# Deformable sampling in a four-layer network: gathered rows as the stationary operand, corner weights as the moving one

## The chip, the cores and the metric

The kernel runs on one core of a Trainium2 chip. A core has engines that run side by side, each through its own list of instructions in order: TensorE for matrix products (PE in the profile; PEld is its loading of the stationary operand), VectorE (DVE), ScalarE (ACT), GpSimd (POOL) and SyncE (SP), which here only starts DMAs. They wait for each other through semaphores. A matrix product takes a stationary operand, which is loaded into the array first, and a moving operand, which is streamed through it column by column; the sum over partitions lands in PSUM[...]. The result's partitions are the columns of the stationary operand, and its columns are those of the moving one.

The metric is the device time of one execution in microseconds (us). Lower is better.

## The reference

Four images of 256 channels and 64x64 pixels go through four layers, each added to its input. Layer 0 holds the part that changes: a deformable convolution. For every pixel, each of four groups of 64 channels has nine points with offsets computed from the data; the image is read at each point by bilinear interpolation (four corners), and the nine values are summed with a softmax mask.

```python
inp = y.transpose(0, 2, 3, 1)
xp = jnp.einsum('nhwc,oc->nhwo', inp, inproj_w) + inproj_b
offset = jnp.einsum('nhwc,oc->nhwo', t, off_w) + off_b
mask = jax.nn.softmax(mlog.reshape(n, H, W, G, P), -1).reshape(n, H, W, G * P)
...
samp = _grid_sample(img, sg)
mr = mask.reshape(n, H * W, G, P).transpose(0, 2, 1, 3).reshape(n * G, 1, H * W, P)
dout = (samp * mr).sum(-1).reshape(n, G * GC, H * W).transpose(0, 2, 1).reshape(n, H, W, C)
dout = jnp.einsum('nhwc,oc->nhwo', dout, outproj_w) + outproj_b
x2 = _bn(inp + dout, bn2_g, bn2_b, bn2_m, bn2_v, 3)
```

So for one pixel and one group the sampling is a sum of 9 points x 4 corners = 36 rows of 64 channels, each times one number (mask times bilinear weight). The rest is dense: 1x1 convolutions and a feed-forward block in layer 0, linear attention with a 5x5 depthwise convolution in layer 1, a binary 3x3 convolution in layer 2, and attention against a pooled image in layer 3.

## The kernel before

`run` lays the four images out as a pipeline. `sample(n)` is the sampling of image n, and is the backbone of four stages: sampling 0 beside the convolutions and offsets of images 1 to 3; sampling 1 beside the feed-forward (`feed`) and layer 1 (`linear`) of image 0; sampling n (2 and 3) beside `feed` and `linear` of image n-1 and layers 2 and 3 (`second`) of image n-2. What is left of images 2 and 3 comes after as a tail without sampling. All these are Python generators, and `beside` interleaves them by hand: after each step of the sampling it advances the others by their share of estimated cost. Within the stages, `ordered()` makes the order of the program the order on TensorE, VectorE, ScalarE and GpSimd. Nothing is rearranged at run time: an instruction that waits holds back all that stand behind it on its engine.

The sampling goes by *rounds* of 14 pixels (`RP`), each with nine points, so 126 of 128 partitions hold one (pixel, point) pair. 293 rounds make an image. Two rounds make a *unit* (`UR`), four share one tile of weights (`WR`), and sixteen are a *block* (`BR`) of 224 pixels, after which the output projection runs.

- `load` (L572) brings a block's table indices and corner weights into `sl` by two DMAs of SP.
- `weigh` (L583) spreads the weights on VectorE into `wm`: for each (pixel, point) row and each group and corner, 16 columns (`OB`) that are zero but for the row's own pixel. So a product of `wm` with gathered rows sums the nine points of every pixel.
- `gathered` (L596) starts four indirect DMAs on GpSimd (L600), one for each group. Each brings to every partition one row of 256 numbers: four corners of 64 channels. The tile `g` has seven buffers. Then eight matmuls follow (L607), for two pairs of corners `x` and four groups `i`, with two corners and 16 columns of `wm` as the stationary operand (128 rows x 32 columns) and two corners' channels of `g` as the moving one (128 columns). Group i's sum goes to partitions 32i to 32i+31 of the accumulator `acc`: pixels (for two corners) in partitions, channels in columns. Of the 32x128 results of a group, those where the stationary's corner is the moving's corner are of use. Each fp32 matmul shows as two passes in the profile, so sixteen records a round.
- `moved` (L610) copies a unit's accumulator from PSUM to SBUF (`at`, ScalarE, L612).
- `turned` (L614) transposes each round's 128x128 on TensorE into a second PSUM bank, `dp` (L617), which puts channels into partitions.
- `spread` (L619) copies the useful halves on ScalarE (L632) from `dp` to `dT`, where all of a block's pixels lie side by side.
- `project` (L636), `add` and `finish` (L642 to L649) are the output projection of the block from `dT`, the sum with the image, and the batch norm.

The main loop (L654 on) issues the matmuls of a round, and puts off what follows: `todo` gives each of `moved`, `turned` and `spread` a step at which it is issued. For a unit whose last round is step i these are i+1, i+2 and i+3 (i+4 in a block's first unit). PSUM is shared out by names: `acc` and `dp` are one bank each, of two halves used in turn by units:

```python
        def halves(name):

            t = self.ps1.tile([P, 2, 256], F32, name=name, tag=name)
            return cycle([t[:, 0], t[:, 1]])

        accs, dps = halves("acc"), halves("dp")
```

The framework derives the waits from tiles, and both halves of a bank are one tile. In the tail the two banks serve other work.

Of the kernel before, what the change touches and what calls it, by code (L numbers as in the profile page):

```python
# [9 lines left out]
F32 = mybir.dt.float32  # L10
# [7 lines left out]
P = 128  # L18
# [5 lines left out]
G, PT = 4, 9  # L24
# [5 lines left out]
RP, WR, UR, BR = 14, 4, 2, 16  # L30
RS, BP = RP * PT, RP * BR
BLOCKS = [(p0, min(BP, HW - p0)) for p0 in range(0, HW, BP)]
OB = 16
# [38 lines left out]
class Net:  # L72
# [483 lines left out]
    def sample(self, n, ssum):  # L556

        nc, sp = self.nc, self.sp
        table = self.tab[n].rearrange("g y x s c -> (g y x) (s c)")
        blocks, images, at, dp, dT, po, later = {}, {}, {}, {}, {}, {}, {}

        def halves(name):

            t = self.ps1.tile([P, 2, 256], F32, name=name, tag=name)
            return cycle([t[:, 0], t[:, 1]])

        accs, dps = halves("acc"), halves("dp")  # L570

        def load(b):  # L572
            p0, np_ = BLOCKS[b]
            whole, part = np_ // RP, np_ % RP

            nr = whole + (part > 0)
            sl = sp.tile([P, BR, G * 5], F32, name="sl")
            rows = self.s_d[n][p0 * PT:p0 * PT + nr * RS, :].rearrange("(r p) f -> p r f", p=RS)
            more = self.s_d[n][p0 * PT + RS:p0 * PT + (nr + 1) * RS, :].rearrange("(r p) f -> p r f", p=RS)
            nc.sync.dma_start(sl[0:RS, 0:nr], rows)  # L580
            nc.sync.dma_start(sl[RS:P, 0:nr], more[0:P - RS])
            rounds = [(r, RP) for r in range(whole)] + [(whole, part)] * (part > 0)
            blocks[b] = sl, rounds  # L583

        def weigh(b, r):

            sl, rounds = blocks[b]
            nu = min(WR, len(rounds) - r)
            wm = self.gp.tile([P, WR, 4 * G, OB], F32, name="wm")
            sh = [P, nu, 4 * G, OB]  # L590
            nc.vector.tensor_tensor(  # L591
                wm[:, 0:nu], self.con("own").unsqueeze(1).unsqueeze(1).to_broadcast(sh),
                sl[:, r:r + nu, G:].unsqueeze(3).to_broadcast(sh), ALU.mult)
            return wm

        def gathered(sl, wm, acc, r):  # L596
            r4, acc = r % WR, acc[:, r % UR * P:(r % UR + 1) * P]
            g = self.gp.tile([P, G, 256], F32, name="g", bufs=7)
            for i in range(G):
                nc.gpsimd.indirect_dma_start(  # L600
                    out=g[:, i, :], out_offset=None, in_=table,
                    in_offset=bass.IndirectOffsetOnAxis(ap=sl.bitcast(I32)[:, r, i:i + 1], axis=0))


            for x in range(2):
                for i in range(G):
                    nc.tensor.matmul(acc[32 * i:32 * i + 32, :], wm[:, r4, 4 * i + 2 * x:4 * i + 2 * x + 2, :],  # L607
                                     g[:, i, x * P:(x + 1) * P], start=x == 0, stop=x == 1)

        def moved(acc, nu, u):  # L610
            at[u] = sp.tile([P, UR, P], F32, name="at")
            nc.scalar.copy(at[u].rearrange("p v c -> p (v c)")[:, 0:nu * P], acc[:, 0:nu * P])  # L612

        def turned(nu, u):  # L614
            dp[u] = next(dps).rearrange("p (v g s o) -> p v g s o", v=UR, g=G, s=2)
            for v in range(nu):
                nc.tensor.transpose(dp[u][:, v].rearrange("p g s o -> p (g s o)"), at[u][:, v], self.ident)  # L617

        def spread(unit, b, u):  # L619

            if b not in dT:
                p0, np_ = BLOCKS[b]
                dT[b] = sp.tile([P, G, BP], F32, name="dT", bufs=1)
                images[b] = sp.tile([P, KT, BP], F32, name="yb")
                nc.sync.dma_start(images[b][:, :, 0:np_], self.y_d[n][:, :, p0:p0 + np_])
            full = sum(1 for _, m in unit if m == RP)
            for v0, v1, m in ((0, full, RP), (full, len(unit), unit[-1][1])):
                for s in range(2):
                    if v0 < v1:
                        hs = slice(64 * s, 64 * s + 64)  # L630
                        q0 = RP * (unit[0][0] + v0)
                        nc.scalar.copy(  # L632
                            dT[b][hs, :, q0:q0 + m * (v1 - v0)].rearrange("p g (v o) -> p g v o", o=m),
                            dp[u][hs, v0:v1, :, s, 0:m].rearrange("p v g o -> p g v o"))

        def project(b, m):  # L636
            np_ = BLOCKS[b][1]
            po[m] = self.ps("po")
            for k in range(G):
                nc.tensor.matmul(po[m][:, 0:np_], self.ow[:, k, m * P:(m + 1) * P], dT[b][:, k, 0:np_], start=k == 0, stop=k == G - 1)  # L640

        def add(b, m):  # L642
            ym = images[b][:, m, 0:BLOCKS[b][1]]
            nc.vector.tensor_tensor(ym, po[m][:, 0:BLOCKS[b][1]], ym, ALU.add)

        def finish(b, m):
            p0, np_ = BLOCKS[b]
            ym = images[b][:, m, 0:np_]
            nc.scalar.activation(ym, ym, AF.Identity, bias=self.sh[:, 4 + m:5 + m],  # L649
                                 scale=self.inv[:, 4 + m:5 + m], accum_out=ssum[:, m, b:b + 1])  # L650
            if m == KT - 1:
                nc.sync.dma_start(self.x2_d[n][:, :, p0:p0 + np_], images[b][:, :, 0:np_])

        load(0)  # L654
        order = [(b, r) for b, (_, np_) in enumerate(BLOCKS) for r in range(-(-np_ // RP))]
        wm = weigh(0, 0)
        for i, (b, r) in enumerate(order):
            for f in later.pop(i, ()):
                f()
            sl, rounds = blocks[b]  # L660
            if r % UR == 0:
                acc = next(accs)
            gathered(sl, wm, acc, r)
            if r == 0 and b + 1 < len(BLOCKS):
                load(b + 1)
            ends = r + 1 == len(rounds)
            if r % WR == 0:
                if r + WR < len(rounds):
                    nxt = weigh(b, r + WR)
                elif b + 1 < len(BLOCKS):  # L670
                    nxt = weigh(b + 1, 0)
            if r % UR == UR - 1 or ends:
                unit = rounds[r - r % UR:r + 1]
                todo = [partial(moved, acc, len(unit), i), partial(turned, len(unit), i), partial(spread, unit, b, i)]

                todo = [(i + 1 + j + (j == 2 and r < UR), f) for j, f in enumerate(todo)]
                if ends:
                    todo += [(i + 4 + m + j, partial(f, b, m)) for m in range(KT) for j, f in enumerate((project, add, finish))]
                for j, f in todo:
                    later.setdefault(j, []).append(f)  # L680
            if r % WR == WR - 1 or ends:
                wm = nxt
            yield 1
        for i in sorted(later):
            for f in later[i]:
                f()
# [656 lines left out]
```

## Time and profile before

| | before |
|---|---|
| median of 3 runs | 8817.04 us (8797.73 to 8818.68) |
| span of the profiled execution | 8805.8 us |
| mean granted TensorE clock | 0.809 of full |
| DMA | 1042.27 MB, mean 118 GB/s |
| first and last matmul of the sampling start at | 139.6 and 7330.2 us |
| first matmul of the sampling of images 0, 1, 2, 3 | 140, 1951, 3718, 5537 us |

Of the granted clock the records know two values, half and full, so a mean of 0.809 says for what share of the time it was full. A line of groups reads: source line, engine, operation, output<-inputs by the program's names, shape (stationary and moving operands for TensorE), count | busy us, mean ns of one | idle us of the engine just before them, and what ended most of it. In a line of the timeline, the brackets at the end hold the idle time before and what ended it; "remote" is a semaphore that was raised where no record of another engine ends, and "issue" is time in which the engine waited for nothing that the profile shows. A line of waits gives the us in total, the times and the longest.

### The profile page before, as it was taken

How to read it: one execution, taken by the hardware profiler on the slowest of the kernel's cores; microseconds unless marked ns; L12 is line 12 of the kernel's file. 1: busy time of each engine (PE TensorE's matmuls, PEld its weight loads, DVE VectorE, ACT ScalarE, POOL GpSimd, SP SyncE). 2: the span in 40 equal slices, each digit the busy share in tenths (PEclk: the TensorE clock that was granted, in tenths of full speed). 3: DMA queues.
4: the chain of work that ended last, by engine and by line, in shares of the span. 5: the costliest groups of instructions: out<-in, count | busy, mean ns of one | idle time of the engine just before them, and what ended most of it. 6: DMA issues, size and time to landing. Idle time of an engine off the chain costs nothing. (4 is left out here: it accounts for less than half of the span.)

```text
span 8805.8 us, 95736 instructions
## 1 busy us (share of the span) xinstructions
PE 5993.9 (68%) x36532; PEld 3575.6 (41%) x36532; DVE 5173.3 (59%) x6409; ACT 2183.8 (25%) x4899; POOL 5152.4 (59%) x4950
## 2 busy tenths in 40 slices
PE   4454554448744446688876677888766778986899
PEld 2222222224323322244544443345544433664477
DVE  5444443443466667424777776227777772599834
ACT  1111111112211112122223222222222222465524
POOL 2666666566666666666666656666666661376410
PEclk7676766669866667799988888898878888998999
DMA  6454454444433334444443344444434343220131
GB/s 172 127 155 124 141 154 118 125 145 145 153 105 105 110 105 129 127 130 138 134 135 110 112 121 136 142 134 132 136 115 117 114 118 99 69 74 29 48 98 53
DMA packets 759050, 1042.27 MB, mean 118 GB/s; under 512 B 362432, under 2 KB 472128, under 8 KB 757056
## 3 DMA queue, kind: packets, MB, share of 16 engines
q0 software_dynamic: 225024, 614.77, 24.3%
q1 hardware_dynamic: 533568, 421.39, 16.4%
q8 instruction: 289, 4.73, 0.2%
q14 instruction: 169, 1.38, 0.0%
HBM read 867.08 MB, written 168.69 MB: 118 GB/s over the span
## 5 line engine op out<-in xcount | busy, mean ns | idle before, releaser
L600 POOL DMA_INDIRECT g<-tab,sl x4688 | 4618.5, 985 | 2687.8 <-issue 1224.2
L178 DVE SCALAR_TENSOR_TENSOR agg<-pad,vec,agg 128x1024 f32<-128x1024 f32 x2280 | 2933.5, 1287 | 61.9
L607 PE MATMUL acc<-g,wm 128*32 128x128 f32 x18752 | 1034.8, 333 | 1907.8 <-ACT at L612 1273.7
L607 PEld LDWEIGHTS acc<-g,wm 128*32 128x32 f32 x18752 | 566.8, 128 | 2411.7 <-ACT at L612 1446.1
L1048 PE MATMUL ps<-xd,w 128*128 128x256 f32 x3072 | 752.7, 396 | 51.3 <-issue 37.8
L591 DVE TENSOR_TENSOR wm<-con,sl 128x1024 f32<-128x1024 f32 (+1 forms) x296 | 357.7, 1209 | 711.9 <-remote 533.5
L1048 PEld LDWEIGHTS ps<-xd,w 128*128 128x128 f32 x3072 | 595.1, 199 | 175.0 <-issue 86.0
L632 ACT COPY dT<-dp 64x112 f32<-64x112 f32 x1176 | 285.9, 243 | 1043.7 <-remote 544.3
L742 PE MATMUL ps<-x2f,f 128*128 128x512 f32 x1024 | 499.2, 636 | 19.1 <-issue 7.7
L817 PE MATMUL ps<-xr,qw 128*128 128x512 f32 x768 | 472.0, 746 | 22.1 <-issue 11.1
L727 DVE SCALAR_TENSOR_TENSOR hm<-ps,vec,lk 128x512 f32<-128x512 f32 x256 | 190.8, 750 | 492.9 <-ACT lk L744 405.5
L752 PE MATMUL ps<-hm,f 128*128 128x512 f32 x1024 | 467.1, 605 | 0.9 <-DVE hm L727 0.9
L612 ACT COPY at<-acc 128x256 f32<-128x256 f32 (+1 forms) x588 | 218.3, 371 | 986.3 <-remote 753.2
L999 POOL TENSOR_TENSOR xd<-xp 128x640 f32<-128x640 f32 x64 | 79.4, 1268 | 492.6 <-ACT xp L1011 298.3
L640 PE MATMUL po<-dT,ow 128*128 128x224 f32 (+1 forms) x1216 | 326.1, 419 | 45.4 <-issue 19.3
L617 PE MATMUL dp<-ident,at 128*128 128x128 f32 x1172 | 284.1, 330 | 106.6 <-ACT dT L632 61.0
L865 ACT COPY kt<-pt 128x512 f32<-128x512 f32 x256 | 149.4, 584 | 829.3 <-remote 403.8
L744 ACT ACTIVATE lk<-ps,low 128x512 f32<-128x512 f32 x256 | 174.0, 687 | 666.0 <-PE ps L742 512.1
L1147 PE MATMUL s<-ph,th 128*128 128x512 f32 x512 | 290.2, 672 | 62.5 <-ACT kt L865 15.9
L640 PEld LDWEIGHTS po<-dT,ow 128*128 128x128 f32 x1216 | 265.5, 233 | 113.8 <-issue 68.9
L1167 PEld LDWEIGHTS ps<-gt,pT 128*128 128x128 f32 x2048 | 276.0, 213 | 70.8 <-issue 46.1
L194 POOL TENSOR_TENSOR ak<-ak,m 128x1024 f32<-128x1024 f32 x96 | 228.1, 2376 | 130.6 <-ACT m L193 126.7
(243 smaller groups left out, 8022.0 us busy)
## 6 DMA issues: line engine op xcount, KB each, us to landing
g<-tab,sl POOLq DMA_INDIRECT x4688
x<-x SPq DMA_DIRECT2D x128, 512.0 KB
xr<-x SPq DMA_DIRECT2D x96, 512.0 KB
tab<-xo SPq DMA_DIRECT2D x192, 128.0 KB
x<-in_x SPq DMA_DIRECT2D x32, 512.0 KB
y<-yc SPq DMA_DIRECT2D x32, 512.0 KB
x2f<-x SPq DMA_DIRECT2D x32, 512.0 KB
xyf<-x SPq DMA_DIRECT2D x32, 512.0 KB
```

Source lines behind the costliest of these rows:

```text
L178: nc.vector.scalar_tensor_tensor(to, s, wt, acc, ALU.mult, ALU.add)
L591: nc.vector.tensor_tensor(wm[:, 0:nu], self.con("own").unsqueeze(1).unsqueeze(1).to_broadcast(sh), sl[:, r:r + nu, G:].unsqueeze(3).to_bro ...
L600: nc.gpsimd.indirect_dma_start(out=g[:, i, :], out_offset=None, in_=table, in_offset=bass.IndirectOffsetOnAxis(ap=sl.bitcast(I32)[:, r, i: ...
L607: nc.tensor.matmul(acc[32 * i:32 * i + 32, :], wm[:, r4, 4 * i + 2 * x:4 * i + 2 * x + 2, :], g[:, i, x * P:(x + 1) * P], start=x == 0, st ...
L617: nc.tensor.transpose(dp[u][:, v].rearrange("p g s o -> p (g s o)"), at[u][:, v], self.ident)
L632: nc.scalar.copy(dT[b][hs, :, q0:q0 + m * (v1 - v0)].rearrange("p g (v o) -> p g v o", o=m), dp[u][hs, v0:v1, :, s, 0:m].rearrange("p v g ...
L640: nc.tensor.matmul(po[m][:, 0:np_], self.ow[:, k, m * P:(m + 1) * P], dT[b][:, k, 0:np_], start=k == 0, stop=k == G - 1)
L742: nc.tensor.matmul(ps, f1[:, k, m * P:(m + 1) * P], x2[:, k], start=k == 0, stop=k == KT - 1)
L752: nc.tensor.matmul(ps, f2[:, k, m * P:(m + 1) * P], hm[:, k], start=k == 0, stop=k == 4 * KT - 1)
L817: nc.tensor.matmul(ps, qw[:, k, m * P:(m + 1) * P], x[:, k], start=k == 0, stop=k == KT - 1)
L1048: nc.tensor.matmul(ps[:, e], w[:, k, t, 2 * half + e, m * P:(m + 1) * P], v[:, 2 * half + e, k, t:t + 8], start=i % 6 == 0, stop=i % 6 == 5)
L1147: nc.tensor.matmul(s[i], tv[:, 4 * b + j], ph[:, i * 512:(i + 1) * 512], start=True, stop=True)
```

## The change

The two operands of the sampling's matmul change places. The gathered rows of one group and one pair of corners (128 rows x 128 columns) are loaded as the stationary operand, and the 32 columns of `wm` move. The sum then comes out with corners and channels in partitions and pixels in columns, which is the layout that `turned` made. So `moved` and `turned` go, and `spread` reads the accumulator itself. A round now fills 4 groups x 32 = 128 columns on all 128 partitions. The order of the loops turns from corner pairs outside to groups outside, so that the two matmuls that add up into one place follow each other. The two PSUM banks both serve as accumulators, each in two halves, and successive units take a half of `acc`, a half of `dp`, the other half of `acc`, the other half of `dp`. `spread` is issued at the same step as before. Gathers, weights, projection and everything beside the sampling are unchanged.

```diff
-        blocks, images, at, dp, dT, po, later = {}, {}, {}, {}, {}, {}, {}
-
-        def halves(name):
-
-            t = self.ps1.tile([P, 2, 256], F32, name=name, tag=name)
-            return cycle([t[:, 0], t[:, 1]])
-
-        accs, dps = halves("acc"), halves("dp")
+        blocks, images, dT, po, later = {}, {}, {}, {}, {}
+        banks = [self.ps1.tile([P, 2, UR, G, 2, OB], F32, name=tag, tag=tag) for tag in ("acc", "dp")]
+        accs = cycle([t[:, i] for i in range(2) for t in banks])
...
-            r4, acc = r % WR, acc[:, r % UR * P:(r % UR + 1) * P]
+            r4, acc = r % WR, acc[:, r % UR]
...
-            for x in range(2):
-                for i in range(G):
-                    nc.tensor.matmul(acc[32 * i:32 * i + 32, :], wm[:, r4, 4 * i + 2 * x:4 * i + 2 * x + 2, :],
-                                     g[:, i, x * P:(x + 1) * P], start=x == 0, stop=x == 1)
-
-        def moved(acc, nu, u):
-            at[u] = sp.tile([P, UR, P], F32, name="at")
-            nc.scalar.copy(at[u].rearrange("p v c -> p (v c)")[:, 0:nu * P], acc[:, 0:nu * P])
-
-        def turned(nu, u):
-            dp[u] = next(dps).rearrange("p (v g s o) -> p v g s o", v=UR, g=G, s=2)
-            for v in range(nu):
-                nc.tensor.transpose(dp[u][:, v].rearrange("p g s o -> p (g s o)"), at[u][:, v], self.ident)
-
-        def spread(unit, b, u):
+            for i in range(G):
+                for x in range(2):
+                    nc.tensor.matmul(acc[:, i], g[:, i, x * P:(x + 1) * P],
+                                     wm[:, r4, 4 * i + 2 * x:4 * i + 2 * x + 2, :], start=x == 0, stop=x == 1)
+
+        def spread(acc, unit, b):
...
-                            dp[u][hs, v0:v1, :, s, 0:m].rearrange("p v g o -> p g v o"))
+                            acc[hs, v0:v1, :, s, 0:m].rearrange("p v g o -> p g v o"))
...
-                todo = [partial(moved, acc, len(unit), i), partial(turned, len(unit), i), partial(spread, unit, b, i)]
-
-                todo = [(i + 1 + j + (j == 2 and r < UR), f) for j, f in enumerate(todo)]
+                todo = [(i + 3 + (r < UR), partial(spread, acc, unit, b))]
```

## The prediction

> **What bounds the kernel now.** I read the page first: the busy shares, then the slices, then the groups of the sampling lines.
>
> ```profile
> PE 5993.9 (68%) x36532; PEld 3575.6 (41%) x36532; DVE 5173.3 (59%) x6409; ACT 2183.8 (25%) x4899; POOL 5152.4 (59%) x4950
> ...
> POOL 2666666566666666666666656666666661376410
> PEclk7676766669866667799988888898878888998999
> ...
> L600 POOL DMA_INDIRECT g<-tab,sl x4688 | 4618.5, 985 | 2687.8 <-issue 1224.2
> ...
> L607 PE MATMUL acc<-g,wm 128*32 128x128 f32 x18752 | 1034.8, 333 | 1907.8 <-ACT at L612 1273.7
> L607 PEld LDWEIGHTS acc<-g,wm 128*32 128x32 f32 x18752 | 566.8, 128 | 2411.7 <-ACT at L612 1446.1
> ...
> L612 ACT COPY at<-acc 128x256 f32<-128x256 f32 (+1 forms) x588 | 218.3, 371 | 986.3 <-remote 753.2
> ...
> L617 PE MATMUL dp<-ident,at 128*128 128x128 f32 x1172 | 284.1, 330 | 106.6 <-ACT dT L632 61.0
> ```
>
> No engine is full, yet POOL shows the same 6 in nearly every slice from the second to the 33rd: the sampling runs at one pace for 7190 us (first L607 at 139.6, last at 7330.2) and everything else is laid beside it. It has 4 x 293 = 1172 rounds of four gathers, so 6.13 us a round. A gather costs 0.985 us, and unhindered ones start 1.25 us apart (0.95 and an idle 0.30 put down to "issue"). With the few of some 2 us, a round that nothing holds takes 5.16 us, and the 293 rounds of an image 1512 us. What POOL loses beyond that, about 1150 us, is the most that any edit of the sampling can return while POOL gathers like this.
>
> Who holds POOL? The table of windows, cut at each image's first L607 (columns: us; busy and count of PE, PEld, DVE, ACT, POOL; clock; DMA share; GB/s), and PE's largest wait in each of these windows, in the same order:
>
> ```profile
> 140.00:1951.00 1811.00, 854.91 (x6748) 492.11 (x6750) 793.18 (x1059) 251.13 (x699) 1186.14 (x1193) 0.65 0.48 136
> 1951.00:3718.00 1767.00, 1056.27 (x6898) 554.53 (x6898) 1051.74 (x1051) 347.27 (x888) 1162.77 (x1176) 0.74 0.42 124
> 3718.00:5537.00 1819.00, 1366.94 (x8673) 818.98 (x8669) 1147.14 (x1373) 453.97 (x1108) 1144.50 (x1172) 0.87 0.44 128
> 5537.00:7330.00 1793.00, 1351.88 (x8634) 808.62 (x8630) 1142.77 (x1365) 449.76 (x1092) 1120.42 (x1144) 0.86 0.43 124
> ```
>
> ```profile
> PE acc L607 <- ACT at L612: 487.7, 71, 27.6
> ...
> PE acc L607 <- ACT at L612: 423.2, 89, 15.1
> ...
> PE acc L607 <- ACT at L612: 182.4, 63, 10.9
> ...
> PE acc L607 <- ACT at L612: 180.6, 59, 11.6
> ```
>
> The reader should see that PE waits for the copy L612 in every stage, and that PE grows from 47% busy to 75%: the four stages last nearly the same, but the later two have far less room. The timeline shows the wait at work:
>
> ```profile
> 1013.63 0.37 ACT L612 COPY at<-acc 128x256 f32<-128x256 f32 x1 [5.35 <-remote]
> 1013.81 0.94 POOL L600 DMA_INDIRECT g<-tab,sl  x1 [2.02 <-remote]
> 1014.06 0.63 PEld L607 LDWEIGHTS acc<-g,wm 128*32 128x32 f32 x16 [7.30 <-ACT at L612]
> 1014.06 1.08 PE L607 MATMUL acc<-g,wm 128*32 128x128 f32 x16 [6.01 <-ACT at L612]
> ```
>
> The two halves of a unit's accumulator bank are one tile to the waits, so the first matmul of a unit waits for the copy of the unit just before; that copy waits for PE. POOL's next gather into the seven g buffers waits for PE in turn ("remote" and "PE acc L607" together 1119.0 us of POOL's idle time over the run).
>
> [...] the mean load is 0.128 us in L607 (32 columns) and 0.199 in L1048 (128). [...] the records know only 0.5 and 1.0 here, and the table shows the mean rise with PE's share, .65 to .87. [...] the sixteen passes of a round of L607 take 0.64 us at full clock and the 1.08 seen above at half. [...]
>
> **The change, part by part.** *Removed:* 586 units' copies L612 (218.3 us of ACT, which is 25% busy, so worth nothing by itself), the transposes L617 (284.1 us of PE), the tiled matmuls L607 (1034.8), and the wait for the copy of the unit before. By stage the two PE lines leave 389, 338, 297 and 294 us.
>
> *Added:* the same 18752 passes, now with 128 stationary columns and 32 moving. The nearest rows are L1167 (128x128 stationary, 128 moving) and L144 (one moving column). Record by record, starts of successive passes are 0.111 to 0.112 us apart for both at full clock and 0.213 at half, so the load sets the pace and moving columns below 128 come free. In a window of the tail at clock 1.00 L1167 takes 39.07/320 = 0.122 us a pass, little above:
>
> ```profile
> 8700.00:8800.00 100.00, 39.07 (x320) 38.65 (x320) 1.00 0.16 53
> ```
>
> A round costs PE 16 x 0.112 = 1.79 us (full) or 3.41 (half), where L607 and L617 cost 0.64+0.38 or 1.08+0.69. From below, a pass could cost 0.111 at any clock; from above 0.213, with the array's clock low. I take a blend, 1.79+1.62 x 2(1-c) at mean clock c.
>
> *Moved:* the spread copies (L632, 1176 of 0.243 us, now from acc) stay as many and as large. The unit's first matmul now waits for the spread of two units earlier, since the halves alternate between the banks; a unit lasts 12.3 us, so this wait should be over when PE comes to it. Where it isn't, the works laid beside the sampling stand behind it in PE's order, as they do now. POOL's and SP's instructions are the same in number and order.
>
> *The sum.* Each stage is as long as the larger of POOL's floor, with some 85 us of remaining stalls (1600), and PE's work plus those waits of PE that the change doesn't touch. These waits are the stage less PE's busy time less the wait for L612: 468, 288, 270 and 260 us. With more work on PE its partners have more time, so part of them goes; I bound what stays by half and by all, and take the middle. The clock should rise with PE's share: I take .80, .85, .95, .95.
> - Stage 0: PE without sampling 502 x .65/.80 = 408, passes 293 x 2.44 = 715, waits 351: 1474. POOL decides: 1600, -211.
> - Stage 1: 765 x .74/.85 = 666, 293 x 2.28 = 668, waits 216: 1550. POOL: 1600, -167.
> - Stage 2: 1126 x .87/.95 = 1031, 293 x 1.95 = 571, waits 135 to 270: 1737 to 1872, middle 1805, -14.
> - Stage 3: 1115 x .86/.95 = 1009, 571, waits 130 to 260: 1710 to 1840, middle 1775, -19.
>
> Together -411. The profiled span is 8805.8, its execution close to the median of 8817.04; 8395 of span is about 8406, say 8400. What is late next is the gathers themselves in stages 0 and 1, PE in 2 and 3. The tail after 7330 has no sampling and stays.
>
> **The rivals.**
> *A, PE keeps room.* If nothing of the other waits stays in the late stages, they are 1602 and 1580, at POOL's pace like the first two: some -800, 8000. For it: PE's completions of L607 are seen by ACT and POOL about 1.2 us after its records end, often 3 to 10, while in the tail each is within 0.02; if that belongs to the tiled form, it goes with it. Against: PE would have to be over 95% busy for 3400 us beside dependent work.
> *B, slower: the clock does not follow.* One mechanism: a new pass streams 32 columns where the array was used on 128, so PE is busy with loads that may not hold the clock up. At the old clocks (.65, .74, .87, .86) passes cost 857, 771, 647 and 657 us: stages 502+857+351 = 1710, 765+771+216 = 1752, 1126+647+202 = 1975, 1115+657+195 = 1967; sum +213, 9020; with .80 in the last two some 9330. With the main case's gain in stages 0 and 1 (-378), the balance tips where stages 2 and 3 exceed 2000 each, at a clock below about .86. For it: the added work is nearly all loads, and PE is 75% busy there already. Against: L1167, half of it loads, runs at 1.00.
> *C, nothing moves.* The late completions belong to the gathers' landing, the ring stays full for that reason, and the copy was only where PE's lateness was seen: 8800, give or take 80. Against: unhindered gathers keep 1.25 us for long stretches.
>
> **How the numbers follow.** Main .40, A .20, B .28, C .12. A measurement of this kernel can tell 0.3% (26 us) from no change. Faster: .36 + .20 + .05 = .61; same: .01 + .05 = .06; slower: .03 + .28 + .02 = .33. The main case's own range is 8160 to 8640 (stages 2 and 3 +-67 each, 0 and 1 together +-100). Leaving out a quarter of A and half of B, the range is 8000 to 9050, as the unknown clock has both signs.
>
> **What would show it.** Lines L612 and L617 gone, PE's wait for them too; 18752 passes at 128 columns with about 2 us of PE a round; ACT some 218 us less; POOL at 5.3 to 5.5 us a round in the first two stages, 6.1 in the last two; the clock at .95 there. Wrong it is if the clock in stages 2 and 3 is .87 or less with PE over 90% busy (B), if POOL still waits for PE in the first two stages (C), or if PE's idle time in the last two all but vanishes (A).

## The result, and the profile after

The changed kernel takes 9220.44 us (median of 4 runs, 9218.42 to 9271.9), the kernel before beside it 8817.86: a ratio of 1.0461 with a 95% interval of 1.0433 to 1.0489. It is slower. The profiled span is 9220.6 us, 414.8 more than before.

The runs fell on two kinds of chip, called the first and the second here, on which the kernel before takes about 8820 and 7740 us; every kernel is compared with the kernel before that ran beside it, and the profile of before and the result above are from the first. Where the record numbers the chips, it has 5, 9 and, in the last two runs, 1 for the first kind, and 4 and 1 for the second. So the number 1 stands on both sides, and whether a kind is a property of a chip or a condition that one chip can be in is not known.

The page of the changed kernel, with the busy shares, the granted clock and the groups of the sampling:

```profile
PE 7778.5 (84%) x35360; PEld 5909.3 (64%) x35360; DVE 5176.7 (56%) x6409; ACT 1984.8 (22%) x4311; POOL 5149.0 (56%) x4950
...
PEclk7565655669755566798977777999877788998899
...
L595 POOL DMA_INDIRECT g<-tab,sl x4688 | 4615.2, 984 | 3091.9 <-issue 1222.3
...
L602 PEld LDWEIGHTS acc<-wm,g 128*128 128x128 f32 x9408 | 1526.3, 248 | 667.4 <-issue 318.9
L602 PE MATMUL acc<-wm,g 128*128 128x32 f32 x9408 | 1527.7, 322 | 479.9 <-issue 225.5
L602 PEld LDWEIGHTS dp<-wm,g 128*128 128x128 f32 x9344 | 1525.0, 252 | 609.1 <-ACT dT L618 299.7
L602 PE MATMUL dp<-wm,g 128*128 128x32 f32 x9344 | 1523.0, 325 | 427.9 <-ACT dT L618 240.2
```

TensorE is busy 84% in place of 68%. The copy and the transposes are gone, the 18752 passes are now 9408 into one bank and 9344 into the other, and together they keep PE busy for 3050.7 us where L607 and L617 took 1318.9. Yet the clock line has more 5s and 6s than before. The windows between the first sampling matmuls of the images (144, 1986, 3834, 5803 and the end, 7741; columns as before):

```profile
144.00:1986.00 1842.00, 1374.74 (x6467) 1188.85 (x6467) 796.78 (x1067) 207.55 (x560) 1197.80 (x1196) 0.59 0.47 134
1986.00:3834.00 1848.00, 1571.47 (x6579) 1186.14 (x6578) 1046.73 (x1042) 294.34 (x733) 1157.35 (x1172) 0.69 0.40 117
3834.00:5803.00 1969.00, 1743.60 (x8376) 1322.72 (x8376) 1148.86 (x1372) 403.12 (x961) 1141.77 (x1172) 0.83 0.40 118
5803.00:7741.00 1938.00, 1718.02 (x8353) 1307.47 (x8354) 1145.52 (x1366) 398.41 (x946) 1113.49 (x1144) 0.84 0.39 115
```

The stages grew by 31, 81, 150 and 145 us: 407 of the 415. The tail takes 1479, and 1476 before. In every stage the mean clock is lower than before (.65, .74, .87, .86) although PE is busier. PE's largest waits over the whole run:

```profile
PE dp L602 <- ACT dT L618: 240.2, 82, 9.4
PE acc L602 <- issue: 225.5, 227, 4.7
PE acc L602 <- ACT dT L618: 201.0, 91, 16.2
```

The wait for the unit just before (1273.7 us) is gone, but 441.2 us of waiting for the spread copies came in, and in the first stage PE is idle for 467 us in all, as long as it was before without the wait at L612 (468).

### The profile page after: what moved, and what is told of

It is laid out like the page before. It is cut to its first block, busy times and chain, and to the rows that moved or that the text cites. A ratio compares the mean times of both kernels' runs of the same rounds, so it can differ in the third digit from the quotient of the medians.

```text
span 9220.6 us, 92659 instructions
## 1 busy us (share of the span) xinstructions
PE 7778.5 (84%) x35360; PEld 5909.3 (64%) x35360; DVE 5176.7 (56%) x6409; ACT 1984.8 (22%) x4311; POOL 5149.0 (56%) x4950
## 5 line engine op out<-in xcount | busy, mean ns | idle before, releaser
L602 PEld LDWEIGHTS acc<-wm,g 128*128 128x128 f32 x9408 | 1526.3, 248 | 667.4 <-issue 318.9
L602 PE MATMUL acc<-wm,g 128*128 128x32 f32 x9408 | 1527.7, 322 | 479.9 <-issue 225.5
L602 PEld LDWEIGHTS dp<-wm,g 128*128 128x128 f32 x9344 | 1525.0, 252 | 609.1 <-ACT dT L618 299.7
L602 PE MATMUL dp<-wm,g 128*128 128x32 f32 x9344 | 1523.0, 325 | 427.9 <-ACT dT L618 240.2
L801 PE MATMUL ps<-xr,qw 128*128 128x512 f32 x768 | 507.3, 796 | 13.1 <-issue 5.2
L1151 PEld LDWEIGHTS ps<-gt,pT 128*128 128x128 f32 x2048 | 314.1, 238 | 67.0 <-issue 39.2
L1151 PE MATMUL ps<-gt,pT 128*128 128x128 f32 x2048 | 324.5, 325 | 7.7 <-ACT pT L1147 6.9
L726 PEld LDWEIGHTS ps<-x2f,f 128*128 128x128 f32 x1024 | 194.5, 198 | 212.0 <-issue 208.8
L736 PEld LDWEIGHTS ps<-hm,f 128*128 128x128 f32 x1024 | 192.5, 194 | 214.8 <-issue 214.8
```

Of the source, the lines that this page charges most:

```text
L602: nc.tensor.matmul(acc[:, i], g[:, i, x * P:(x + 1) * P], wm[:, r4, 4 * i + 2 * x:4 * i + 2 * x + 2, :], start=x == 0, stop=x == 1)
L726: nc.tensor.matmul(ps, f1[:, k, m * P:(m + 1) * P], x2[:, k], start=k == 0, stop=k == KT - 1)
L736: nc.tensor.matmul(ps, f2[:, k, m * P:(m + 1) * P], hm[:, k], start=k == 0, stop=k == 4 * KT - 1)
L801: nc.tensor.matmul(ps, qw[:, k, m * P:(m + 1) * P], x[:, k], start=k == 0, stop=k == KT - 1)
L1151: nc.tensor.matmul(ps[:, 0:P], pT[:, m], gt[:, m], start=m == 0, stop=m == 7)
```

## The experiments

### Breaking the wait alone: e1_banks

This is the kernel before with its accumulators and transposes placed otherwise; nothing else changes.

```diff
-        accs, dps = halves("acc"), halves("dp")
+        banks = [self.ps1.tile([P, 2, 256], F32, name=tag, tag=tag) for tag in ("acc", "dp")]
+        accs, dps = cycle([t[:, 0] for t in banks]), cycle([t[:, 1] for t in banks[::-1]])
```

> The kernel before with nothing changed but the places in PSUM: successive units accumulate in acc and dp by turns (first halves), and the transposes of a unit go to the second half of the other bank, so that the first matmul of a unit no longer waits for the copy of the unit just before. Theory 1 (the stages are PE's busy time plus its waits, and the new orientation lost because a round's loads cost PE 2.2 to 3 us where tiled matmuls and transposes took about 1.1): the wait at L612 falls from 1274 us to under 400, the clock stays, the first two stages fall to about 1600 each and the last two to about 1640, 8050 to 8250 in all. Rival (ACT's place in the order holds PE, whatever the bank): the wait moves to another copy and the time stays within 100 us of 8817. Rival (PE is late because of the gathers): the same, with POOL still waiting for PE.

Measured: 8758.36 us, 0.9923 (0.9893 to 0.9953) of the kernel before. Its stages are 1818, 1751, 1795 and 1768 us (before: 1811, 1767, 1819, 1793). PE's largest waits:

```profile
PE acc L603 <- issue: 380.4, 495, 2.5
PE dp L603 <- issue: 325.8, 424, 8.1
PE dp L613 <- ACT at L608: 178.4, 45, 25.0
...
PE acc L613 <- ACT at L608: 110.9, 27, 14.5
```

The wait went as Theory 1 said: the matmuls no longer have it, and 289 us of it now stand at the transposes. The time of Theory 1 (8050 to 8250) did not come. PE now stands idle at the same matmuls for 706 us waiting for nothing that the profile shows. So the wait for the copy was, for the most part, the place where PE was late, and not the reason; the 289 us that are left are taken up in e7_late below. The time is that of both rivals. The first, that the wait moves to another copy, fits no more than these 289 us.

### Do the moving columns set the clock: e2_mv64 and e3_mv128

Both are the changed kernel with more moving columns to each loaded 128x128. In e2_mv64 a unit takes a bank (`[P, UR, G, 4, OB]`), and the added sums lie beside the needed ones:

```diff
-                    nc.tensor.matmul(acc[:, i], g[:, i, x * P:(x + 1) * P],
-                                     wm[:, r4, 4 * i + 2 * x:4 * i + 2 * x + 2, :], start=x == 0, stop=x == 1)
+                    c = 2 if x and i == G - 1 else 4
+                    nc.tensor.matmul(acc[:, i, 0:c], g[:, i, x * P:(x + 1) * P],
+                                     wm[:, r4, 4 * i + 2 * x:4 * i + 2 * x + c, :], start=x == 0, stop=x == 1)
```

> The changed kernel with 64 moving columns in 7 of the 8 matmuls of a round (the needed 32 and 32 more, whose sums nobody reads), 128 stationary columns as before; a unit then fills a bank, and the wait between units stays that of two units earlier. Theory 1 with the clock (32 moving columns to a 128-column load are too little to keep the granted clock up): a pass at a given clock costs the same, the clock rises by 0.02 to 0.06 in every stage, time 8900 to 9150. If the clock doesn't answer to moving columns: 9220 +-30. If a pass is not set by its load: slower, above 9300.

Measured: 9112.82 us, 1.0314 (1.0283 to 1.0345) of the kernel before, mean clock .803 against .771, and higher by .02 to .06 in every stage, as expected.

In e3_mv128:

```diff
+                    c = min(4 * i + 2 * x, 2 * G)
+                    nc.tensor.matmul(acc.rearrange("p g s o -> p (g s) o"), g[:, i, x * P:(x + 1) * P],
+                                     wm[:, r4, c:c + 2 * G, :], start=i + x == 0, stop=i + x == G)
```

> The changed kernel with 128 moving columns in all eight matmuls of a round, which all add up into one group of 128 columns of the accumulator; so the sampling's sums are not the reference's (groups are mixed), while loads, passes, copies, gathers and waits are the same in number. If moving columns hold the clock up: clock at or above that of the kernel before in each stage (.65, .74, .87, .86), passes still 0.11 us apart at full clock, time 8600 to 8950. If not: clock as in the changed kernel (.59, .69, .83, .84) and 9220 or more.

Measured: 8948.9 us in one run, at the upper end of what was expected, mean clock .874. Its windows, cut in the same way:

```profile
141.00:1975.00 1834.00, 1159.18 (x6469) 947.85 (x6470) 797.06 (x1068) 207.67 (x560) 1196.38 (x1196) 0.75 0.48 135
1975.00:3761.00 1786.00, 1290.25 (x6577) 971.63 (x6577) 1046.54 (x1042) 294.62 (x733) 1161.87 (x1172) 0.84 0.42 122
3761.00:5631.00 1870.00, 1573.09 (x8376) 1200.67 (x8375) 1148.06 (x1372) 402.47 (x961) 1147.88 (x1172) 0.92 0.43 125
5631.00:7476.00 1845.00, 1555.64 (x8353) 1188.32 (x8354) 1145.58 (x1366) 398.10 (x946) 1116.93 (x1144) 0.93 0.42 121
```

The clock answers to the moving columns: .59, .65, .75 in the first stage with 32, 64 and 128 of them, and .83, .85, .92 in the third. Record by record, the starts of passes are 0.111 to 0.112 us apart at full clock and 0.213 at half, with 32 columns as with 128. So four times the columns streamed cost no pass any time, and the clock is faster: .771 over the run with 32 of them, .874 with 128. That is what the prediction's rival B reckoned with. The first stage is as telling in another way: with PE's busy time down by 216 us it lost 8.

### The spread copy in ScalarE's order: e4_early

```diff
-                todo = [(i + 3 + (r < UR), partial(spread, acc, unit, b))]
+                todo = [(i + 2 + (r < UR), partial(spread, acc, unit, b))]
```

> The changed kernel with each unit's spread copies issued one round earlier, so that the first matmul of the unit after next finds them a whole round behind. PE waits 441 us for these copies in the changed kernel. Rival (this coupling with ACT ate the gain): these waits go, 8750 to 8900. Theory 1 (PE's loads set the time, these waits are part of what stays): a third to two thirds of them go, 8950 to 9150.

Measured: 9004.7 us, 1.0195 (1.0166 to 1.0224). That is 216 us less than the changed kernel's 9220, half of the 441; in the profiles the four stages lose 19, 30, 69 and 82 us. That is within Theory 1's range. PE's waits for these copies at L602 fell from 441 to 220 us. In the changed kernel, the spread copy of a unit is issued in the very step in which the unit after next begins. The data had a unit of slack; ScalarE's place in its order had none.

### Fewer passes: e5_x0 and e6_one

```diff
             for i in range(G):
-                for x in range(2):
-                    nc.tensor.matmul(acc[:, i], g[:, i, x * P:(x + 1) * P],
-                                     wm[:, r4, 4 * i + 2 * x:4 * i + 2 * x + 2, :], start=x == 0, stop=x == 1)
+                nc.tensor.matmul(acc[:, i], g[:, i, 0:P], wm[:, r4, 4 * i:4 * i + 2, :], start=True, stop=True)
```

> The changed kernel without the second pair of corners: eight passes a round in place of sixteen, each with its 128-column load; half of the sum over corners is left out. Theory 1 (a stage is PE's busy time plus its other waits, down to what GpSimd's gathers need, about 1600): PE loses 438, 412, 334 and 334 us, stages 1600, 1600, 1640, 1600, in all 8050 to 8250. Rival (a limit of about 1780 a stage that is not PE's passes, since the first two stages took 1751 to 1834 in all runs so far): 8700 to 8800.

Measured: 8829.3 us in one run; stages 1789, 1746, 1841 and 1825. Theory 1 (8050 to 8250) failed by far, and the rival's range was missed by 29 us. Against the changed kernel the first two stages lose 53 and 102 us where PE lost 421 and 410 of busy time.

In e6_one one matmul a round remains:

```diff
+                nc.tensor.matmul(acc.rearrange("p g s o -> p (g s) o"), g[:, G - 1, 0:P], wm[:, r4, 0:2 * G, :], start=True, stop=True)
```

> The changed kernel with one matmul a round in place of eight (two passes of 128 moving columns); all gathers, weights and copies stay, seven eighths of the sampling's sums are left out. Theory 1: POOL's pace sets the first two stages and nearly the others, 1520 to 1620 each, 7750 to 8050 in all. Rival (limit of about 1780 a stage from gathers or from the work beside): 8650 to 8800, with POOL still waiting 250 us or more in each stage.

Measured: 8683.8 us in one run; the rival's number. The first two windows:

```profile
148.00:1917.00 1769.00, 637.36 (x2368) 421.95 (x2367) 792.89 (x1067) 205.92 (x560) 1172.89 (x1188) 0.61 0.48 138
1917.00:3629.00 1712.00, 870.73 (x2474) 481.40 (x2473) 1042.21 (x1041) 294.41 (x733) 1154.83 (x1177) 0.70 0.43 127
```

PE is busy 36% of the first stage and still POOL does not get through its 293 rounds in less than 1769 us. A stretch of the timeline shows what can hold it:

```profile
883.85 3.22 PE L392 MATMUL ps<-iw,yc 128*64 128x256 f32 x16
...
899.15 0.25 PE L494 MATMUL ps<-mw,t 128*128 128x108 f32 x1 [0.92 <-issue]
901.95 0.25 PE L494 MATMUL ps<-mw,t 128*128 128x108 f32 x1 [2.55 <-issue]
904.75 0.34 PE L494 MATMUL ps<-mw,t 128*128 128x108 f32 x1 [2.55 <-issue]
...
914.76 0.94 POOL L595 DMA_INDIRECT g<-tab,sl  x1 [0.30 <-issue]
...
922.27 0.69 DVE L397 TENSOR_TENSOR xo<-ps,rows 128x512 f32<-128x512 f32 x1 [41.74 <-remote]
...
924.85 0.94 POOL L595 DMA_INDIRECT g<-tab,sl  x1 [9.15 <-remote]
```

The matmuls of L392 end at 887.07, and VectorE's L397, which reads their result, starts at 922.27. Between 877.43 and 922.24 no raise of TensorE's semaphore is in the trace, though six instructions that raise it end in between, the last at 905.09. Meanwhile POOL gathers every 1.25 us until its seven buffers are full, and stops at 915.7; TensorE, from 899 on, starts a load or a matmul mostly 0.70 or 1.4 us after the last, waiting for nothing that the profile shows. The next raise of its semaphore in the trace, at 922.24, comes 6.5 us after that stop.

How often are its signals that late on this chip? I counted each TensorE instruction that raises the semaphore as on time if the trace has the raise within 0.15 us of its recorded end, and sorted them by the gathers that POOL had started since its last pause of over 0.7 us (those that end in a pause are left out). In the kernel before, on time were:

```
gathers since the pause   1-2    3-5    6-9    10-14   15-19
TensorE                  0.62   0.36   0.12    0.07    0.00
  of so many              702   1128    704     211      18
```

All 831 of TensorE after the last gather are on time. After POOL's last gather before a pause the next raise of TensorE comes within 1.04 us at the lower quartile and 1.67 at the median. Two limits of this count: the ends of matmuls are modelled in the records, so a signal that is held back and a matmul that completes late look alike here; and the trace has 3713 raises for 3942 such instructions, so up to 229 of those counted as late may only be missing.

For VectorE and ScalarE the same count shows no lateness. Of their 4023 and 2401 raises in the trace all but two of each stand within 0.15 us of a recorded end; for the rest of their 5644 and 3116 instructions that raise a semaphore the trace has no raise at all. So what is shown to come late is TensorE's alone.

### Fewer gathers: e8_half

```diff
-            for i in range(G):
+            for i in range(0, G, 2):
                 nc.gpsimd.indirect_dma_start(
...
-                    nc.tensor.matmul(acc[:, i], g[:, i, x * P:(x + 1) * P],
+                    nc.tensor.matmul(acc[:, i], g[:, i // 2 * 2, x * P:(x + 1) * P],
```

> The changed kernel with two gathers a round in place of four; all sixteen passes stay and read the two gathered parts twice, so two groups take the rows of others. Theory 1: PE sets the time, 9050 to 9200, with stages 2 and 3 within 60 us of 1969 and 1938. Rival (gathers or their transfers limit the first two stages): stages 0 and 1 fall by over 100 us each, and all four if it holds for the others.

Measured: 8252.38 us in one run. Theory 1 (9050 to 9200, the last two stages within 60 us of 1969 and 1938) failed, and the rival held in all four stages.

```profile
140.00:1473.00 1333.00, 1209.06 (x6470) 1055.90 (x6470) 797.66 (x1069) 206.69 (x560) 617.00 (x597) 0.66 0.46 126
1473.00:3122.00 1649.00, 1521.14 (x6577) 1157.75 (x6577) 1045.50 (x1042) 294.73 (x733) 595.36 (x586) 0.72 0.29 85
3122.00:4969.00 1847.00, 1700.42 (x8378) 1291.75 (x8379) 1147.53 (x1373) 402.95 (x961) 570.62 (x586) 0.84 0.29 85
4969.00:6771.00 1802.00, 1659.68 (x8352) 1262.29 (x8352) 1143.05 (x1365) 398.62 (x946) 559.21 (x572) 0.86 0.28 82
```

With all of PE's passes and half the gathers, the stages lose 509, 199, 122 and 136 us against the changed kernel. PE is busy 91 to 92% in each, and of all its signals 84% are on time in the first stage and 98 to 99% in the others. So here PE is the bound at last, and the last two stages (1847 and 1802) are what the changed kernel's PE work takes when nearly all its signals are on time. In the first two stages on the first chip, no edit of PE's passes that was tried got below 1769 and 1712 us with four gathers a round.

Is it the gathers in a row, or the traffic that they make? The amount moved alone does not explain it: the first stage here moves 126 GB/s with 84% of TensorE's signals on time, the second of the kernel before 124 GB/s with 34%. And where e8_half has several gathers in a row, TensorE's signals are late too: on time are 60% of 89 after three to five, and 1 of 12 after six to nine.

### Other orders and buffers: e7_late, e9_ring4, e10_after4

e7_late is e1_banks with the transposes and the spread copies a round later:

```diff
-                todo = [(i + 1 + j + (j == 2 and r < UR), f) for j, f in enumerate(todo)]
+                todo = [(i + (1, 3, 4)[j] + (j == 2 and r < UR), f) for j, f in enumerate(todo)]
```

> The kernel before with units by turns in the two banks (as in e1_banks) and the transposes and spread copies issued one round later, so that the transposes find their copy a round behind. PE waits 289 us there for the copy. Theory 1: half or more of that comes back, 8550 to 8700. Rival (a limit of about 1780 a stage that is not PE's): 8740 to 8780, as e1_banks.

Measured: 8748.63 us, 0.9926 (0.9904 to 0.9948): the rival's number, no more than e1_banks. The wait at the transposes is gone from PE's largest waits, and 881 us of idle time at the matmuls, put down to "issue", and 265 us of waits for the spread copies stand in its place. So here too the place changed and the time did not.

e9_ring4 is the kernel before, and e10_after4 the changed kernel, with `bufs=4` in place of 7 for `g`.

> The kernel before with 4 buffers for the gathered rows in place of 7. Theory 2 (TensorE's completion signals are held back while gathers follow each other without a pause, and come out about 1 us after GpSimd stops; in the kernel before 62% of TensorE's signals are on time within two gathers of a pause, 11% after six to nine): the runs of gathers get shorter, more signals are on time, and the time is no longer than before, 8500 to 8850. Ordinary buffering (seven rounds of lead are needed to cover TensorE's other work): 9000 or more.

> The changed kernel with 4 buffers for the gathered rows in place of 7. Theory 2: 9050 to 9250, more signals on time. Ordinary buffering: 9400 or more, since TensorE is busier here.

These two and the two memset runs below fell on the second chip, where the kernel before takes 7740.75 us and 99% of TensorE's signals are on time. e9_ring4 took 7823.97 us, 1.0111 (1.0094 to 1.0127), so the ring of seven buys about 1% there. e10_after4 took 8436.17 us in one run, as long as the changed kernel with seven there (8437.38, below). Neither tells anything of late signals.

### A short pause for GpSimd: e11_rest and e12_banks_rest

```diff
+            nc.gpsimd.memset(self.gp.tile([P, 64], F32, name="rest"), 0.0)
```

> The kernel before with one small memset on GpSimd after the four gathers of each round (a tile that nobody reads), 1172 more instructions. Theory 2, if anything but a gather counts as a pause: over 80% of TensorE's signals on time while the sampling runs, 8400 to 8750. If only an idle GpSimd lets the signals out: lateness as before and 8820 to 9050.

> The same memset in e1_banks (units by turns in two banks). Theory 2, if it counts as a pause: the gain that e1_banks didn't bring appears, 8250 to 8650. If not: 8760 to 9000.

On the second chip: 7769.33 us, 1.0037 (1.0023 to 1.0051), and 7706.88 us, 0.9956 (0.9940 to 0.9973). With 99% of TensorE's signals on time without the memset, these two do not show what it would do to late ones. The two together give an estimate of e1_banks without the memset on this chip: 0.9956/1.0037, or 0.992, so the other placement alone is worth as little there as on the first.

### Both kernels on the second chip: r1_before, r2_after, r3_rest, r4_ring4

> The kernel before, unchanged, for its trace on this chip. The last four runs were on a chip where it takes 7741 us and where TensorE's signals were on time in 99% of cases. If this chip is like that one: stages of 1520 to 1560 us, TensorE's signals on time. If it is like the first: 8820, as shown.

> The changed kernel, unchanged, beside the kernel before on this chip. Theory 1 (TensorE's loads and the lower clock set the changed kernel's stages; held-back signals hid part of that on the first chip by slowing the kernel before): where the signals are on time the ratio is larger than 1.046, 1.07 to 1.10, with stages of about 1590, 1650, 1800 and 1790. On a chip like the first: 1.046 again.

These ran on the second kind of chip again. r1_before: 7738.35 us in one run. r2_after: 8437.38 us, 1.0915 (1.0890 to 1.0940). The windows of r1_before:

```profile
142.00:1658.00 1516.00, 1005.01 (x6744) 531.77 (x6744) 798.48 (x1059) 252.05 (x699) 1152.20 (x1171) 0.70 0.56 160
1658.00:3191.00 1533.00, 1130.41 (x6895) 569.42 (x6898) 1048.83 (x1051) 349.29 (x888) 1162.86 (x1185) 0.79 0.49 143
3191.00:4728.00 1537.00, 1260.48 (x8670) 770.70 (x8663) 1141.57 (x1373) 454.94 (x1108) 1147.15 (x1174) 0.91 0.52 152
4728.00:6257.00 1529.00, 1257.88 (x8643) 769.50 (x8644) 1138.27 (x1365) 450.95 (x1092) 1125.55 (x1157) 0.91 0.50 147
```

and of r2_after:

```profile
143.00:1697.00 1554.00, 1320.12 (x6471) 1122.18 (x6470) 798.93 (x1068) 207.11 (x560) 1163.10 (x1182) 0.63 0.55 158
1697.00:3315.00 1618.00, 1483.83 (x6575) 1125.67 (x6574) 1044.28 (x1040) 294.73 (x733) 1166.09 (x1186) 0.74 0.46 135
3315.00:5124.00 1809.00, 1662.62 (x8376) 1265.77 (x8376) 1146.38 (x1373) 402.87 (x961) 1145.67 (x1172) 0.86 0.44 129
5124.00:6930.00 1806.00, 1664.62 (x8352) 1262.90 (x8352) 1143.38 (x1366) 398.58 (x946) 1119.94 (x1144) 0.86 0.42 123
```

This is the change where signals come on time. Before, all four stages stand at GpSimd's pace (1512 us was worked out for a stage that nothing holds), with PE at 66 to 82% and 99% of its signals on time, at 143 to 160 GB/s. PE's two largest waits in r1_before are:

```profile
PE acc L607 <- DMA g<-tab,sl: 565.8, 690, 21.2
PE acc L607 <- ACT at L612: 523.7, 315, 14.5
```

So the wait for the copy still stands at 524 us here, and yet the stages are as short as GpSimd's gathers allow. After, the first stage stays near that pace with PE 85% busy; in the other three PE is 92% busy and sets 1618, 1809 and 1806 us. In the last two the clock falls from .91 to .86.

r3_rest and r4_ring4 ask again about a pause and a shorter ring:

> The kernel before with a small memset on GpSimd after each round's gathers. On a chip like the first: theory 2, if anything but a gather counts as a pause, 8400 to 8750 and most signals on time; if only an idle GpSimd does, 8820 to 9050. On a chip where signals are on time: 1.003 to 1.005, as in e11_rest.

> The kernel before with 4 buffers for the gathered rows. On a chip like the first, theory 2: 8500 to 8850, more signals on time than with 7; ordinary buffering: 9000 or more. On a chip where signals are on time: 1.01, as in e9_ring4.

They measured 1.0032 (1.0018 to 1.0047) and 1.0105 (1.0088 to 1.0122), as e11_rest and e9_ring4 had, again on the second kind. Whether a pause or a shorter ring brings the signals on time on a chip like the first is left open.

### Again on the first chip: s1_banks and s2_x0

> The kernel of e1_banks again (the kernel before with units by turns in the two banks). On a chip where TensorE's signals are on time its stages stand at GpSimd's pace already (1516 to 1537 us against 1512 worked out), so at most the tail and some 15 us a stage can go: ratio 0.990 to 0.998. On a chip like the first: 0.992 as before.

> The kernel of e5_x0 again (the changed kernel with eight of its sixteen passes a round; half of the sum over corners is left out). On a chip where signals are on time, theory 1: TensorE loses about 430, 390, 320 and 320 us, all four stages go to GpSimd's pace (1520 to 1580), 7700 to 7850, so nearly the whole loss of the changed kernel there was its loads. If something else in the change costs: above 8000. On a chip like the first: 8830 again.

Both fell on a chip like the first, with the kernel before at 8830.32 us. s1_banks: 8760.95 us, 0.9916 (0.9893 to 0.9939), so e1_banks beats both kernels there by a little, on two occasions. s2_x0: 8837.82 us, 1.0004 (0.9988 to 1.0020). The expectation for a chip like the first held in both. Without half of its passes the changed kernel is level with the kernel before: the loss is gone, and the gain that was forecast doesn't appear.

## Why the prediction was wrong

The forecast of 8400 us and the range to 9050 lie below the 9220 measured. By its own steps:

- **"POOL decides: 1600, -211" and "-167" in stages 0 and 1: this step failed first.** It took POOL's losses beyond its own pace for a result of the wait at L612. With this wait gone the stages measured 1842 and 1848 in the changed kernel and 1818 and 1751 in e1_banks, and with an eighth of the sampling's passes (e6_one, PE 36 and 51% busy) 1769 and 1712. What the runs point to is TensorE's signals that come late while gathers follow each other (in the kernel before 62% on time within two gathers of a pause, 7% after ten to fourteen): with half the gathers (e8_half) the stages fell to 1333 and 1649 under all of PE's passes, and on the second chip, with the same gathers and 99% of the signals on time, the kernel before takes 1516 and 1533. No run brings the signals on time on the first chip and leaves all else alone. Rival C, given .12, had named the late completions and that the copy was only where they were seen; its time of 8800 was wrong, since it gave PE's added work no price. Between the forecast of these two stages (3200) and their measure (3690) lie 490 us; 281 of them are there even in e6_one (3481). The other 209 go with the passes that e6_one leaves out.
- **"The clock should rise with PE's share: I take .80, .85, .95, .95": failed.** It was .59, .69, .83 and .84. The forecast read the clock off the windows of the kernel before, where it went from .65 to .86 as PE's busy share went from 47 to 75%. But a pass that loads 128 columns and streams 32 keeps PE busy in the records and went with a lower clock: with the same loads the mean over the run was .771 with 32 streamed columns, .803 with 64 (e2_mv64) and .874 with 128 (e3_mv128). And the busy share did not foretell it: in the first stage e3_mv128 has a clock of .75 with PE 63% busy, and the changed kernel .59 with PE 75% busy. This is most of the miss in the late stages, 164 and 163 us over the forecast: PE was busy 1744 and 1718 us there in place of 1602 and 1580. Its other work took 1158 and 1131 us, not 1031 and 1009; the passes' own lines show 667 and 669, not 571, of which some 80 lie beside records of other lines.
- **"This wait should be over when PE comes to it": failed.** It took 441 us. About half of it came from the copy's place in ScalarE's order, in the same step: issuing it a round earlier (e4_early) returned 216. What makes the other half wasn't tried; with signals on time (r2_after) the wait is still 350 us.
- **The price of a pass (0.111 and 0.213 us) was right**, as the starts of L602's records show, with 32 moving columns as with 128. The loads have 128 rows and 128 columns in the changed kernel, e2_mv64 and e3_mv128 alike, so what a load of another shape takes these runs don't show.
- **What remains of PE's other waits.** The prediction bounded it by half and all of 468, 288, 270 and 260 us. PE is idle for 467, 277, 225 and 220, but 76, 147, 119 and 100 of these are the new wait at L602 for the spread copies. Without it 392, 130, 107 and 120 are left: most of it in the first stage, a little under half in the others. So the new wait took the place of what was gained.
- **Rival B's arithmetic came closest.** With the old clocks it gave 1710, 1752, 1975 and 1967, and the last two measured 1969 and 1938. That is partly luck: PE's busy time there was 29 and 54 us under B's sum, its idle time 23 and 25 over. The first two are longer by 132 and 96, mostly in idle time (467 and 277 where B had 351 and 216). It was given .28.

On the second chip the prediction's own stages for the changed kernel, 1600, 1600, 1805 and 1775, meet 1554, 1618, 1809 and 1806, and POOL's 1512 us meets 1516 to 1537 of the kernel before. That agreement is partly luck, since a clock taken too high there stood against waits taken too long. But it agrees with the first point: the largest error lay in what the kernel before was waiting for on the first chip.

## What to carry to other kernels

A wait that ends last is the place where lateness shows, and the cheap way to learn whether it is also the cause is to remove it alone (here two lines of buffer placement: a wait of 1274 us went from the matmuls, and 0.8% of the time) before making another engine pay for its removal. Exchanging the operands of this matmul traded columns streamed for columns loaded: 32 and 128 in place of 128 and 32. Price such a pass by rows of the trace with the same load (here 0.111 to 0.112 us at full clock and 0.213 at half, with 32 streamed columns as with 128), and reckon with a lower clock where few columns follow each load (.771 over the run with 32, .874 with 128). When data has a unit of slack, look at the order of the engine that must do the copy too; issuing it one step earlier gave back half of a new wait (441 us became 220).

## What the runs showed of the hardware

- On the first chip TensorE's completion signals come late while GpSimd's indirect gathers follow each other: in the kernel before 62% are on time within two gathers of a pause and 7% after ten to fourteen, and in e6_one VectorE's L397 started 35 us after the recorded end of the matmuls that it reads. In the same stretch TensorE's loads and matmuls start 0.70 or 1.4 us apart. On the second chip 99% of TensorE's signals are on time at the same pace of gathers (1.25 us). Why the chips differ isn't known, nor what makes the signals late, nor whether it is the signal or the matmul that is late. The kernel before is 1080 us longer on the first, all of it in the sampling stages: the tail takes 1476 us there and 1480 on the second.
- With the same loads, the granted clock rose with the columns streamed: .771, .803 and .874 over the run for 32, 64 and 128 moving columns (e2_mv64 has 64 in 7 of 8 matmuls), while PE's busy share of the first stage fell from 75 to 70 and 63%.
- The same change costs 4.6% on the first chip and 9.2% on the second. A likely reading, not tested by itself, is that late signals hid part of TensorE's added work: in the kernel before, TensorE was idle for 25 to 53% of a stage on the first chip and for 18 to 34% on the second.
